# A Mamba-like block with mixture of experts: the token's row is made ready where x1 is made

## The chip, the cores and the metric

The kernel runs on one core of one Trainium2 chip, in float32. The metric is the device time of one execution in microseconds, as the median of the runs; smaller is better. The core has five instruction queues that run beside each other, each in its own fixed order: PE (matrix products), DVE and POOL (elementwise work; POOL also issues the indirect DMAs), ACT (functions, scale and bias) and SP (which only issues DMAs here).

## The reference, cut to what matters

Input are 8 sequences of 512 tokens with 256 features. For each sequence six modulation vectors of 256 numbers come from a small product. Two stages follow.

```python
sa, ca, ga, sb, cb, gb = mod vectors of the sequence      # ga, gb kept away from zero
h  = layernorm(x) * (1 + ca) + sa
x1 = x + ga * mixer(h)           # layernorm, W_in, causal conv + silu, linear state scan, gate, W_out, + h
h2 = layernorm(x1) * (1 + cb) + sb
logits = h2 @ wr + br            # 8 experts; top 1; gate = p1 / (p1 + p2)
y  = gelu(h2 @ w1[e] + b1[e]) @ w2[e] + b2[e]             # 256 -> 1024 -> 256, e the token's expert
out = x1 + gb * gate * y
```

The routing is dense in the reference (each expert over all tokens, masked); the kernel computes each token for its own expert alone.

## The kernel before, in words

**Order of the work.** All operations of a stage are first listed in a class `Plan` (lines 36 to 286). `Plan.order` then gives each engine one fixed order: always the operation that can start first by a table of estimated lengths (`length`), among equals the one with the earlier due time (`nc.due`); buffers are given in turn. `emit` issues them in that order. The recorded line of nearly every operation is therefore that of the plan's two helpers, L154 and L159, and operations are told apart by the names of their tiles.

**Stage 1** (lines 431 to 1138) goes over the 8 sequences b; a due time of 36 us per sequence (`PERIOD`) staggers them, so that several sequences overlap. A tile has 128 partitions; 512 tokens are 4 tiles.
- `stage_norm` (735): layer norm of x, modulation (h, on DVE), layer norm again, transposes to xnT (PE and ACT).
- `stage_base` (759): h times ga plus x, and W_out times ga (`wb_`): three 128x1024 operations on POOL.
- `stage_conv` (774): the scan's input pv and its three steps pd, each added to v by DVE; four products px, each copied to u and scaled to sv by ACT; three taps per product on DVE (`sv<-u,pt,sv`, twelve operations per sequence), then silu on ACT.
- `stage_out` (824): four products px for the gate (tz, tanh on ACT), the state's part pc (`v` times `cs`) added to sv by DVE, times the gate; then po (W_out and the router in one product, four tiles), x1 from po, statistics of x1 (`rs` by a power on POOL, `nm` on DVE), the logits, the choice of expert.
- `stage_place` (899): the gate's value, the token's row written to DRAM, and the token's number scattered into the list of its expert (`ids_d`, four indirect DMAs on POOL per sequence).

**The token's row.** `xp_d` in DRAM has one row per token, of `ROW` = 260 + 768 numbers (4112 bytes): x1 (256), rs, nm, gate, 0, and then copies of the sequence's three vectors for stage 2 (1 + cb, sb, gb), which SP copies in DRAM from `modb_d` for a whole sequence at a time (1.5 MB).

**Stage 2** (lines 1139 to 1332) works through slots of 256 tokens of one expert (12 pairs of tiles and 7 single tiles after 4 early slots; the rest behind a condition). Per slot: `name_tokens` (1023) loads the slot's token numbers, `expert_of` (1036) the expert's w1, b1, b2 and w2 (2.1 MB on SP), `rows_of` (1056) gathers the tokens' rows by an indirect DMA per tile on POOL, `features` (1066) computes h2 from the row (`hg`, three DVE operations per tile) and transposes it, `layer1` (1084) does ph and gelu, `layer2` (1260) does py and three DVE operations per tile, and an indirect DMA writes the output rows.

**The early slots.** When 6 sequences are routed, `early_table` (958) chooses 4 slots that are already full. Their token numbers are loaded in stage 1; the rows of slots 0 and 1 are gathered there, their transposed features made, and slot 0's weights loaded, so that `layer1` of slot 0 can follow the last po. The rows of slots 2 and 3 are gathered in stage 2. The table of the other slots is computed by some forty small DVE operations after the last sequence's routing; SP's next token list waits for it, and the weights of slots 2 and 3 stand behind that list in SP's queue.

Of the kernel before, what the change touches and what calls it, by code (L numbers as in the profile page):

```python
# [10 lines left out]
FP = mybir.dt.float32  # L11
# [10 lines left out]
OWN = 260  # L22
# [267 lines left out]
def adaln_mamba_moe_kernel(  # L290
# [89 lines left out]
    for e in range(E):  # L380
        nc.gpsimd.memset(seen[0:1, e : e + 1], float(e * TOK))
# [4 lines left out]
    for i in range(NSLOT):  # L386
        single = i >= NPAIR
        m = i - NPAIR if single else i
        for q, v in enumerate((
            m, NPAIR + m // 2 if single else m, (m % 2) * P if single else 0,  # L390
            0 if single else NSING,
        )):
            nc.gpsimd.memset(sl_at[:, q, i : i + 1], float(v))

    ex_at = cpool.tile([1, 2, 2 * E], FP, name="ex_at")
    for e in range(2 * E):
        nc.gpsimd.memset(ex_at[:, 0, e : e + 1], float(e % E))
        nc.gpsimd.memset(ex_at[:, 1, e : e + 1], float((e % E) * TOK))
# [5 lines left out]
    ROW = OWN + 3 * D  # L404
    ids_d = dpool.tile([NIDS, 1], I32, name="ids_d")
    id_views = dram_disjoint_views(ids_d, NB)
    xp_d = dpool.tile([TOK + BLK, ROW], FP, name="xp_d")
# [6 lines left out]
    xg0 = epool.tile([P, JB, ROW], FP, name="xg0", tag="xg0")  # L414
    zero = xg0[:, 0, :]
# [15 lines left out]
    with tc.tile_pool(name="wa", bufs=1) as wa, tc.tile_pool(  # L431
# [3 lines left out]
    ) as a2, tc.tile_pool(  # L435
        name="rowp", bufs=2
# [27 lines left out]
        cmt = wa.tile([DS, DI], FP, name="cmt")  # L464
# [5 lines left out]
        for j in range(JB):  # L470
            nc.sync.dma_start(out=xp_d[TOK + j * P : TOK + (j + 1) * P, :], in_=zero)
# [41 lines left out]
        def vectors():  # L513

            for half, to in ((0, mod_d), (1, modb_d)):
                mod = wa.tile([B, 3, D], FP, name=f"mod{half}", tag="mod")
                three(mod, sT, half, B)
                nc.sync.dma_start(out=to, in_=mod.rearrange("b i d -> b (i d)"))
# [71 lines left out]
        def states():  # L590
# [18 lines left out]
            lt = wa.tile([DS, CH, P], FP, name="lt")  # L609
# [70 lines left out]
        def stats(src, b, which, rs=None, nm=None):  # L680
# [8 lines left out]
            if rs is None:  # L689
                rs = sm.tile([P, NT], FP, name=f"rs{which}_{b}", tag=f"rs{which}", bufs=2)  # L690
                nm = sm.tile([P, NT], FP, name=f"nm{which}_{b}", tag=f"nm{which}", bufs=2)
# [82 lines left out]
        def stage_conv(t):  # L774
# [30 lines left out]
            sv = a2.tile([P, KI, L], FP, name="sv")  # L805
# [18 lines left out]
        def stage_out(t):  # L824
# [24 lines left out]

            xr = rowp.tile([P, NT, OWN], FP, name="xr")  # L850
            x1 = xr[:, :, 0:D]
            lg = sm.tile([P, NT, E], FP, name="lg")
            for n in range(NT):
                po = ps_o.tile([P, D + E], FP, name="po", tag="po")
                with nc.wanting([xr]):
# [13 lines left out]
            rs, nm = stats(x1, b, 2, xr[:, :, D], xr[:, :, D + 1])  # L869
# [27 lines left out]
            t.update(xr=xr, top=top, oh=oh)  # L897

        def stage_place(t):

            b, xr, top, oh = (t[k] for k in ("b", "xr", "top", "oh"))
# [3 lines left out]
            nc.vector.tensor_scalar(  # L905
                xr[:, :, D + 2], gt[:, :, 0], 0.5, 0.5, ALU.mult, ALU.add
            )
            nc.vector.memset(xr[:, :, D + 3 : OWN], 0.0)
            nc.sync.dma_start(
                out=xp_d[b * L : (b + 1) * L, 0:OWN].rearrange("(n p) c -> p n c", p=P), in_=xr  # L910
            )
            for n in range(b + 1 if b else 0, min(b + 2, B)):
                nc.sync.dma_start(
                    out=xp_d[n * L : (n + 1) * L, OWN:ROW], in_=modb_d[n].partition_broadcast(L)
                )

# [96 lines left out]
        def tiles(i):  # L1013
            return JB if i < NEARLY + NPAIR else 1
# [41 lines left out]
        def rows_of(i, xg, upto):  # L1056

            for j in range(tiles(i)):
                nc.gpsimd.indirect_dma_start(
                    out=xg[:, j, :], out_offset=None, in_=xp_d[0:upto, :],  # L1060
# [5 lines left out]
        def features(i, xg, hg, hT, tp):  # L1066

            mg = xg[:, :, OWN:ROW]
            for j in range(tiles(i)):
                nc.vector.tensor_scalar(  # L1070
                    hg[:, j, :], xg[:, j, 0:D], xg[:, j, D : D + 1], xg[:, j, D + 1 : D + 2],
                    ALU.mult, ALU.add,
                )
# [315 lines left out]
```

## Time and profile before

| | |
|---|---|
| runs | 588.8, 591.74, 591.7 us; median 591.7 |
| profiled execution | 587.33 us, its span 585.2 us |
| granted TensorE clock | 0.987 (mean over the span) |
| busy: PE, DVE, ACT, POOL | 562.3, 348.1, 211.0, 209.3 us |
| share of the chain that ended last | PE 73%, DMA 17%, DVE 3%, issue 3% |
| moved by DMA | 96.73 MB, 23.17 MB of it by POOL's queue (gathers, scatters) |
| po of the sequences begins at | 70.2, 105, 140, 173, 205, 238, 272, 305 us |

How to read it: the durations and the places come from the one profiled execution, whose time of 587.33 us is its span and what lies around it. An engine's row in a timeline gives the start, the duration, the engine, the line (a helper's), the operation with output and inputs, and in brackets how long the engine was idle before it and what released it. Operations of one engine overlap a little, so a row of a sequence is slightly longer than its share of the time. "sv" is also the buffer of y2; "h" that of the base; "xr" the row of x1 with rs, nm and gate.

### The profile page before, as it was taken

How to read it: one execution, taken by the hardware profiler on the slowest of the kernel's cores; microseconds unless marked ns; L12 is line 12 of the kernel's file. 1: busy time of each engine (PE TensorE's matmuls, PEld its weight loads, DVE VectorE, ACT ScalarE, POOL GpSimd, SP SyncE). 2: the span in 40 equal slices, each digit the busy share in tenths (PEclk: the TensorE clock that was granted, in tenths of full speed). 3: DMA queues.
4: the chain of work that ended last, by engine and by line, in shares of the span. 5: the costliest groups of instructions: out<-in, count | busy, mean ns of one | idle time of the engine just before them, and what ended most of it. 6: DMA issues, size and time to landing. Idle time of an engine off the chain costs nothing.

```text
span 585.2 us, 8673 instructions
## 1 busy us (share of the span) xinstructions
PE 562.3 (96%) x2882; PEld 428.0 (73%) x2882; DVE 348.1 (59%) x1087; ACT 211.0 (36%) x404; POOL 209.3 (36%) x330
## 2 busy tenths in 40 slices
PE   4999999999999999999999798999999999999996
PEld 2454766757576676757578687878988988988895
DVE  4879968798987968686595924163433433522312
ACT  2328454455363445252342021222422222332140
POOL 1423673635446372621333421342242222322112
PEclk9779999999999999999999999999999999999999
DMA  7348999420210101010553969997887787886000
GB/s 277 129 129 183 271 254 258 71 91 0 64 38 1 38 2 36 1 37 1 161 175 91 239 198 398 394 396 266 282 279 275 274 251 242 276 286 194 15 18 20
DMA packets 58703, 96.73 MB, mean 165 GB/s; under 512 B 9852, under 2 KB 41854, under 8 KB 58656
## 3 DMA queue, kind: packets, MB, share of 16 engines
q1 hardware_dynamic: 50720, 72.98, 41.4%
q0 software_dynamic: 7936, 23.17, 11.1%
q8 instruction: 24, 0.39, 0.3%
q14 instruction: 23, 0.19, 0.2%
HBM read 86.42 MB, written 22.81 MB: 187 GB/s over the span
## 4 chain that ended last, share of the span: by engine, by line
PE 73%; DMA 17%; DVE 3%; issue 3%; SPq 1%; POOL 1%; ACT 0%; POOLq 0%; ACTq 0%
PE py L154 10%; PE px L159 10%; PE po L154 9%; PE px L154 9%; DMA out<-ot,ids 8%; PE ph L159 6%; PE ph L154 6%; PE pc L154 3%; PE po L159 3%; PE pd L154 3%; DMA ids<-ids_d 3%; DMA ids_d<-tok,row 2%; DMA w1t<-in_w 2%; PE py L159 2%; DMA xg<-xp_d,ids 1%
## 5 line engine op out<-in xcount | busy, mean ns | idle before, releaser
L159 ACT ACTIVATE gl<-ph,b1t 128x256 f32<-128x256 f32 (+1 forms) x152 | 68.3, 452 | 179.5 <-PE ph L154 159.9
L154 PE MATMUL py<-w2t,gl 128*128 128x256 f32 x476 | 108.3, 379 | 0.0
L154 PEld LDWEIGHTS py<-w2t,gl 128*128 128x128 f32 x476 | 90.4, 190 | 12.3
L159 PE MATMUL ph<-hT,w1t 128*128 128x256 f32 (+1 forms) x304 | 84.1, 358 | 5.4 <-DMA w1t<-in_w 3.0
L154 PE MATMUL ph<-hT,w1t 128*128 128x256 f32 (+1 forms) x304 | 83.8, 357 | 0.0
L159 POOL DMA_INDIRECT out<-ot,ids x36 | 36.4, 1012 | 130.7 <-DVE ot L159 121.0
L159 DVE TENSOR_TENSOR ot<-py,b2t 128x256 f32<-128x256 f32 x34 | 14.4, 424 | 113.0 <-PE py L154 113.0
L159 DVE SCALAR_TENSOR_TENSOR sv<-u,pt,sv 128x512 f32<-128x512 f32 x96 | 71.9, 759 | 4.3 <-ACT sv L159 4.3
L159 POOL DMA_INDIRECT xg<-xp_d,ids x36 | 38.9, 1080 | 87.3 <-DMA ids<-ids_d 48.3
L159 PE MATMUL px<-xnT,wi 128*128 128x512 f32 x128 | 69.6, 625 | 0.0
L154 PE MATMUL px<-xnT,wi 128*128 128x512 f32 x128 | 66.2, 599 | 0.0
L159 PEld LDWEIGHTS ph<-hT,w1t 128*128 128x128 f32 x304 | 54.4, 190 | 12.2 <-issue 3.6
L154 PEld LDWEIGHTS ph<-hT,w1t 128*128 128x128 f32 x304 | 55.3, 190 | 6.2
L154 PEld LDWEIGHTS px<-xnT,wi 128*128 128x128 f32 x128 | 24.6, 192 | 31.2 <-issue 31.2
L159 POOL DMA_INDIRECT ids_d<-tok,row x32 | 34.5, 1077 | 24.2 <-DVE row L159 13.2
L159 ACT COPY u<-px 128x512 f32<-128x512 f32 x32 | 18.7, 585 | 67.0 <-PE px L154 66.4
L159 ACT ACTIVATE tz<-px 128x512 f32<-128x512 f32 x32 | 19.0, 595 | 51.1 <-PE px L154 50.3
L159 POOL TENSOR_TENSOR rs<-ve,nhalf 128x4 f32<-128x4 f32 x16 | 18.8, 1174 | 44.9 <-DVE ve L159 32.2
L159 PEld LDWEIGHTS px<-xnT,wi 128*128 128x128 f32 x128 | 21.3, 192 | 17.4 <-issue 16.5
L159 DVE COPY hT<-tp 128x512 f32<-128x512 f32 (+1 forms) x20 | 12.7, 634 | 35.4 <-PE tp L154 27.4
L159 DVE TENSOR_TENSOR xr<-po,h 128x256 f32<-128x256 f32 x32 | 13.5, 423 | 30.6 <-PE po L154 30.4
L159 DVE TENSOR_TENSOR hg<-hg,xg 128x256 f32<-128x256 f32 x72 | 29.3, 421 | 1.1
(347 smaller groups left out, 949.8 us busy)
## 6 DMA issues: line engine op xcount, KB each, us to landing
w1t<-in_w SPq DMA_DIRECT2D x19, 1024.0 KB
w2t<-in_w SPq DMA_DIRECT2D x19, 1024.0 KB
xp_d<-modb_d SPq DMA_DIRECT2D x8, 1536.0 KB
xp_d<-xr SPq DMA_DIRECT2D x8, 520.0 KB
xt<-in_x SPq DMA_DIRECT2D x8, 512.0 KB
bc<-mod_d SPq DMA_DIRECT2D x7, 384.0 KB
b2t<-in_b SPq DMA_DIRECT2D x19, 128.0 KB
w<-in_w SPq DMA_DIRECT2D x2, 1024.0 KB
```

The costliest lines, as they stand in the source:

```text
L154: me["calls"].append(lambda: getattr(getattr(self.nc, name), op)(*args, **kw))
L159: calls=[lambda: getattr(getattr(self.nc, name), op)(*args, **kw)],
```

## The change

The row becomes three times 256 numbers (3072 bytes): x1, h2, and gate times gb. It is made in stage 1:

- `stage_place` writes x1 by itself, loads the sequence's three vectors into all partitions (`bb`, 384 KB), and makes h2 (four ACT operations `normed` of 128x256, then two POOL operations of 128x1024: times 1 + cb, plus sb) and gate times gb (`gg`, four ACT operations). Both lie in the buffer of `sv`, which has a pool of its own now and is held until the two rows are written. Their due time is a period later.
- The last sequence's two writes are issued in stage 2, behind the weights of slot 1.
- The copies of vectors in DRAM are gone.
- `features` transposes from the gathered row; `hg` is gone. `layer2` does two DVE operations of 128x512 per slot ahead of py (gate gb b2, added to x1), and two per tile after it.
- The rows of all four early slots are gathered in stage 1, one after the other on POOL.
- Constant tables come from counters and copies in place of single memsets; some small tiles change their pools; `layer1` of slot 0 is due a period earlier.

```diff
-    ROW = OWN + 3 * D
-    xp_d = dpool.tile([TOK + BLK, ROW], FP, name="xp_d")
+    xp_d = dpool.tile([TOK + BLK, 3 * D], FP, name="xp_d")
...
+        name="yp", bufs=2
+    ) as yp, tc.tile_pool(
...
-            sv = a2.tile([P, KI, L], FP, name="sv")
+            sv = yp.tile([P, KI, L], FP, name="sv")
...
-            b, xr, top, oh = (t[k] for k in ("b", "xr", "top", "oh"))
+            b, sv, x1, rs, nm, top, oh = (
+                t[k] for k in ("b", "sv", "x1", "rs", "nm", "top", "oh")
+            )
+            own = xp_d[b * L : (b + 1) * L].rearrange("(n p) (i d) -> i p n d", p=P, i=3)
+            nc.sync.dma_start(out=own[0], in_=x1)
             gt = sm.tile([P, NT, 1], FP, name="gt")
             nc.vector.tensor_tensor(gt, top[:, :, 0:1], top[:, :, 1:2], ALU.subtract)
             nc.scalar.activation(gt, gt, AF.Tanh, scale=0.5)
-            nc.vector.tensor_scalar(
-                xr[:, :, D + 2], gt[:, :, 0], 0.5, 0.5, ALU.mult, ALU.add
-            )
-            nc.vector.memset(xr[:, :, D + 3 : OWN], 0.0)
+            nc.vector.tensor_scalar(gt, gt, 0.5, 0.5, ALU.mult, ALU.add)
...
+            h2, gg = (
+                sv[:, k * KD : (k + 1) * KD, :].rearrange("p k l -> p (k l)").rearrange(
+                    "p (n d) -> p n d", n=NT
+                ) for k in range(2)
+            )
+            bb = rowp.tile([P, 3, D], FP, name="bb", bufs=1)
             nc.sync.dma_start(
-                out=xp_d[b * L : (b + 1) * L, 0:OWN].rearrange("(n p) c -> p n c", p=P), in_=xr
-            )
-            for n in range(b + 1 if b else 0, min(b + 2, B)):
-                nc.sync.dma_start(
-                    out=xp_d[n * L : (n + 1) * L, OWN:ROW], in_=modb_d[n].partition_broadcast(L)
-                )
+                out=bb, in_=modb_d[b].rearrange("(i d) -> i d", d=D).partition_broadcast(P)
+            )
+
+            nc.due += PERIOD
+            normed(h2, x1, rs, nm)
+            nc.gpsimd.tensor_tensor(h2, h2, rows(bb[:, 0, :]), ALU.mult)
+            nc.gpsimd.tensor_tensor(h2, h2, rows(bb[:, 1, :]), ALU.add)
+            if b < B - 1:
+                nc.sync.dma_start(out=own[1], in_=h2)
+            for n in range(NT):
+                nc.scalar.activation(
+                    gg[:, n, :], bb[:, 2, :], AF.Identity, scale=gt[:, n, :]
+                )
+            if b < B - 1:
+                nc.sync.dma_start(out=own[2], in_=gg)
+            else:
+                late.extend(((own[1], h2), (own[2], gg)))
+            nc.due -= PERIOD
...
-        def features(i, xg, hg, hT, tp):
-            mg = xg[:, :, OWN:ROW]
+        def features(i, xg, hT, tp):
             for j in range(tiles(i)):
-                nc.vector.tensor_scalar(
-                    hg[:, j, :], xg[:, j, 0:D], xg[:, j, D : D + 1], xg[:, j, D + 1 : D + 2],
-                    ALU.mult, ALU.add,
-                )
-                nc.vector.tensor_tensor(hg[:, j, :], hg[:, j, :], mg[:, j, 0:D], ALU.mult)
-                nc.vector.tensor_tensor(hg[:, j, :], hg[:, j, :], mg[:, j, D : 2 * D], ALU.add)
                 for k in range(KD):
                     nc.tensor.transpose(
-                        tp[:, k, j * P : (j + 1) * P], hg[:, j, k * P : (k + 1) * P], ident
+                        tp[:, k, j * P : (j + 1) * P], xg[:, j, 1, k * P : (k + 1) * P], ident
                     )
...
+                for i in range(NEARLY):
+                    pre.append(rows_of(
+                        i, epool.tile([P, JB, 3, D], FP, name=f"xg_{i}", tag=f"xg{i}"), (b + 1) * L
+                    ))
                 for i in range(2):
...
-                    pre.append(rows_of(
-                        i, epool.tile([P, JB, ROW], FP, name=f"xg_{i}", tag=f"xg{i}"), (b + 1) * L
-                    ))
...
-        nc.due = (B + 4) * PERIOD
+        nc.due = (B + 3) * PERIOD
...
         got = [slot0, fetched(1, pre[1])]
+        for to, v in late:
+            with nc.wanting(done=[got[1][4]]):
+                nc.sync.dma_start(out=to, in_=v)
...
+            nc.vector.tensor_tensor(
+                ot[:, 0:jb], gg, b2t.unsqueeze(1).to_broadcast([P, jb, D]), ALU.mult
+            )
+            nc.vector.tensor_tensor(x1, x1, ot[:, 0:jb], ALU.add)
             for j in range(tiles(i)):
...
-                nc.vector.tensor_tensor(ot[:, j, :], py, b2t, ALU.add)
-                nc.vector.tensor_tensor(ot[:, j, :], ot[:, j, :], mg[:, j, 2 * D : 3 * D], ALU.mult)
-                nc.vector.scalar_tensor_tensor(
-                    ot[:, j, :], ot[:, j, :], xg[:, j, D + 2 : D + 3], xg[:, j, 0:D],
-                    ALU.mult, ALU.add,
-                )
+                nc.vector.tensor_tensor(ot[:, j, :], py, gg[:, j, :], ALU.mult)
+                nc.vector.tensor_tensor(ot[:, j, :], ot[:, j, :], x1[:, j, :], ALU.add)
...
-        got += [fetched(i, None, [ids[:, NEARLY, :]]) for i in range(2, NEARLY)]
+        got += [fetched(i, pre[i], [ids[:, NEARLY, :]]) for i in range(2, NEARLY)]
```

## The prediction

> **What bounds the kernel now.** I read the page first (busy shares, slices, chain), then a table of stretches, then the engines' timelines. PE is busy 562.3 of 585.2 us, and the table shows where it is not:
>
> ```profile
> core 0: us, PE busy (x) PEld busy (x) DVE busy (x) ACT busy (x) POOL busy (x), PEclk, DMA share, GB/s
> ...
> 140.00:173.00 33.00, 33.00 (x179) 22.53 (x178) 29.92 (x93) 15.77 (x29) 16.30 (x26) 1.00 0.15 45
> ...
> 206.00:239.00 33.00, 32.99 (x177) 22.45 (x176) 24.99 (x77) 15.72 (x29) 15.59 (x27) 1.00 0.06 17
> ...
> 315.00:330.00 15.00, 14.01 (x69) 12.04 (x67) 11.92 (x74) 3.89 (x9) 8.90 (x9) 1.00 0.87 263
> 330.00:345.00 15.00, 12.79 (x61) 10.83 (x62) 8.28 (x26) 3.47 (x8) 3.86 (x4) 1.00 0.71 126
> ```
>
> Two things are to be seen. From 105 us to the end of stage 1 PE has no hole to speak of, so nothing taken off another engine there can shorten the run; but DVE is at 25 to 30 of 33 us, so something put on DVE can lengthen it. The only holes of some size that the change can reach lie at the passage to stage 2, where PE waited three times:
>
> ```profile
> 329.94 0.67 PE L159 MATMUL ph<-hT,w1t 128*128 128x256 f32 x2 [0.99 <-DMA w1t<-in_w]
> 335.84 0.70 PE L159 MATMUL ph<-hT,w1t 128*128 128x256 f32 x2 [2.21 <-ACT gl L159]
> 356.88 0.67 PE L159 MATMUL ph<-hT,w1t 128*128 128x256 f32 x2 [2.04 <-DMA w1t<-in_w]
> ```
>
> The second is a DMA too: ACT's gelu had waited for the bias b1t. From 390 to 570 us PE is full (180.00 of 180.00).
>
> **The change, gains first.** PE's instructions stay. *Passage.* The gathers of slots 2 and 3 (before issued at 314.75 to 320.7, 2.1 MB) move into stage 1, behind those of slots 0 and 1; the weights of slot 1, issued at 319.06, then have the DMA to themselves: the 0.99 and 2.21 us go. Transposes no longer wait for DVE's hg and what followed it at 383 to 388 (0.3 + 0.8 us). The wait of 2.04 us for slot 3's weights I keep: they follow the late table, its token list and slot 2's weights on SP, and the table's last operations now also follow slot 0's output operations on DVE; it may go, or double. A routing matmul (pk) stands earlier in PE's queue, some 0.3 us to pay. *Tail.* After the last py (579.45) DVE does two operations instead of three: 0.48 us (row: the scaled add, 482 ns). Sum: 0.99 + 2.21 + 1.1 + 0.48 - 0.3 = 4.5 us gained, bounds 0.5 and 6.5.
>
> *What is worth nothing.* Stage 2's DVE work per slot falls from 5.8 to 3.7 us: PE covers it. Gathers of 3072 instead of 4112 bytes and no copies of modulation rows (8 x 1.5 MB, which fill the DMA at 0.94 to 0.98 in 45 to 105 us): PE's losses there, 1.7 us, are mostly startup waits for small tables, not these; 0 to 0.5 us, taken as 0. Some 100 memsets of 89 ns leave POOL's idle time. Per sequence SP now issues x1, the load bb, h2 and gg (1.9 MB) for 2.0 MB before: DMA share there is 0.05 to 0.26, hidden.
>
> *ACT.* Eight 128x256 operations per sequence: the row xn<-h,nm,rs x4 is 2.08 us, so 4.2 us on top of about 16 of 33. They stand between the copies of px, where ACT idled 0.45 us between pairs and 2.4 us before the first tz; what PE needs next (u, tz) is late by at most one of them. Nothing, or 0.5 us a sequence if that cover is gone.
>
> *POOL.* Two 128x1024 operations of 2.36 us per sequence (h2 times, plus), 4.7 us, on 16 of 33. By itself this fits. Behind them stand the four scatters of token numbers, 1 to 3 us later, which nobody needs but the early table of sequence 5 (ids issued at 279.22, some 2 us late, slot 0 not before 314) and of sequence 7. All eight early gathers (1.3 us apart) stand before h2 of sequence 6, which so comes at 295 to 300; SP, in order, holds slot 0's weights behind that write, to 300 instead of 292.21. They took about 12 us and are wanted at 314: 2 us of cover.
>
> **What decides: where POOL's new operations fall.** Before, POOL's 128x1024 operations lie beside po, when DVE mostly reads PSUM. Where one does meet a DVE operation with two operands in SBUF, the timelines of POOL and DVE show this:
>
> ```profile
> 64.20 2.36 POOL L159 TENSOR_TENSOR h<-h,bc 128x1024 f32<-128x1024 f32 x1 [0.56 <-ACT xn L159]
> 117.56 2.64 POOL L159 TENSOR_TENSOR wb__431<-wo,bc 128x1024 f32<-128x1024 f32 x1
> 149.97 2.36 POOL L159 TENSOR_TENSOR wb__507<-wo,bc 128x1024 f32<-128x1024 f32 x1
> ```
>
> ```profile
> 64.77 0.69 DVE L159 TENSOR_TENSOR sv<-sv,pc 128x512 f32<-128x512 f32 x1 [0.21 <-PE pc L154]
> 65.38 1.72 DVE L159 SCALAR_TENSOR_TENSOR sv<-tz,sv 128x512 f32<-128x512 f32 x1
> 117.89 2.34 DVE L159 SCALAR_TENSOR_TENSOR xr<-mv,xr 128x4 f32<-128x4 f32 x1
> 150.73 2.67 DVE L159 TENSOR_TENSOR h<-xn,bc 128x1024 f32<-128x1024 f32 x1
> ```
>
> An operation on four elements, otherwise 0.15 us, took 2.34 us and ended just when POOL's did (120.2); the one at 65.38, otherwise 0.68, lasted until 66.56 + 0.6; the one at 150.73, otherwise 1.21, until 152.33 + 1.1. The one at 64.77 with pc from PSUM was not held up. The Trainium skill has this as a rule (SBUF — State Buffer, "Who interferes with whom"): a VectorE instruction with two SBUF inputs and a GpSimd instruction that reads SBUF share a port, and whichever comes second is blocked for the whole of the first. It speaks against this change, and the group's row would hide it:
>
> ```profile
> L159 DVE SCALAR_TENSOR_TENSOR sv<-u,pt,sv 128x512 f32<-128x512 f32 x96 | 71.9, 759 | 4.3 <-ACT sv L159 4.3
> ```
>
> By this mean of 759 ns the convolution's twelve operations cost after what they cost before, and the sum is -4.5 us, 587. By the rule each of POOL's two h2 operations takes up to 2.36 us out of DVE if it starts among them. In the changed kernel's instruction order it does: ACT makes h2's norm behind nm and the gate's tanh, some 10 us after po, and POOL's pair follows at once; DVE is then at the seventh or eighth of the twelve. I take the rule's value, as the near rows show it whole.
>
> Followed through once, for the sequence whose po ended at 213.3 (times of before):
>
> ```profile
> 226.28 0.27 DVE L159 TENSOR_TENSOR v<-v,pd 32x120 f32<-32x120 f32 x1
> ...
> 230.15 0.23 DVE L159 TENSOR_TENSOR v<-v,pd 32x96 f32<-32x96 f32 x1
> ```
>
> ```profile
> 228.45 0.35 PE L159 MATMUL pd<-v,lm 32*32 32x96 f32 x2
> ...
> 231.59 0.39 PE L159 MATMUL pc<-v,cs 128*128 128x128 f32 x2
> ```
>
> ACT ends px's last pair at 223.0, tanh and three norms by 224.9; POOL multiplies from about 225.4 (a running DVE operation ends first) to 227.8, adds to 230.2. Between, DVE gets one operation in at most. So v<-v,pd moves from 226.5 to 231.2, and PE, which wants it for pd at 228.45, stands 2.75 us. Three statistics operations of h now stand ahead of the convolution instead of behind it (two more, 0.7 us): 3.4 us. The next sum of v (234.7) then just meets pc, but y2's last operations end some 0.6 us after PE's last cover before po: 4.0. So 2.75 to 4.0 us in which PE is idle; I take the middle, 3.4. In the fuller stretch from 140 the slack was less (v's last sum ended at 164.0, pc began at 164.43), in the one from 281 some DVE work on hg is gone but the pair falls on the last four of the twelve. So 3.4 us for each of six sequences, 20.4. The first has its routing ahead of its convolution and scatters between the two POOL operations: 0.5. The last collides with the tables of stage 2, whose end waits for py anyway: 0.
>
> **Sum.** 20.4 + 0.5 - 4.5 = +16.4 us. Its base is the profiled execution (587.33 us, of which the span is 585.2); the median of the runs shown is 591.7, 4.4 above, and the difference is carried over: 608.1, 2.8% slower.
>
> **Rivals.**
> *A, the likeliest (0.73):* the block stands, 608. With 2 us per sequence (the pair starts later and meets PSUM operations) 599.5; with all 4.7 us lost and little gained at the passage, 617. Its own range is 599 to 617.
> *B, no block that PE feels (0.13):* POOL's operations wait in DVE's gaps, or DVE catches up. For it: the DVE gap of 1.10 us before pc at 232.75, and that at 117.56 POOL itself waited 0.29 us. Against: in three rows above POOL was never put off longer. It decides if DVE is held under about 2 us before v's second sum (226.5 against 228.45); then the passage's gain stays: 591.7 - 4.5 = 587.
> *C, half of it (0.09):* one of the two operations is caught by slack, 1 us per sequence: 6 + 0.5 - 4.5 = +2, 594, and 591 to 599 with its bounds.
> *D, another slower cause (0.05):* h2 of sequence 6 is so late that slot 0's weights come after 314; the cover of 2 us gone, PE waits some 5 us at the first ph, on top of B or C: 592 to 599. For it: SP's fixed order. Against: the 14 us between issue and need.
> That the change misses its aim at the passage (weights again behind a token list) costs A 2 to 4 us, inside its range.
>
> **Numbers.** Less than 0.5% (3 us) can't be told from no change here. Faster: B, 0.13. The same: a third of C and of D, 0.05. Slower: 0.82. The range leaves out B and the top of A: 592 to 617.
>
> **What would show it.** Right: several sv<-u,pt,sv of 2.4 to 3 us beside POOL's sv<-sv,bb, the group's mean above 0.9 us; PE idle some 3 us before pd or pc in each stage-1 sequence, put down to DVE v; po every 36 to 37 us instead of 33.4; POOL's rows of 128x1024 at about 2.36; no waits at the first ph of slot 1. Wrong: a po period near 33.4, with sv<-u at 759 ns, or PE's idle time put down to ACT or to weights.

## The result, and the profile after

The changed kernel takes 622.4 us (median of four runs, 619.7 to 630.7) beside 590.3 us for the kernel before (585.7 to 591.7): a ratio of 1.054, 95% interval 1.045 to 1.064. The forecast was 608, with a range of 592 to 617. One of the four runs (630.7) fell in a slower state of the chip; such runs are left out of the ratios here and below, though not out of the medians. The direction was right; the loss is twice the one forecast. The profiled execution took 620.29 us, its span is 618.6 us, 33.4 us longer than before's 585.2.

First the page's busy times and slices, of before and then of after (each digit is a fortieth of the span; PEclk is the granted TensorE clock in tenths):

```profile
PE 562.3 (96%) x2882; PEld 428.0 (73%) x2882; DVE 348.1 (59%) x1087; ACT 211.0 (36%) x404; POOL 209.3 (36%) x330
...
PE   4999999999999999999999798999999999999996
...
PEclk9779999999999999999999999999999999999999
```

```profile
PE 578.4 (93%) x2882; PEld 437.4 (71%) x2882; DVE 362.6 (59%) x979; ACT 239.1 (39%) x468; POOL 253.3 (41%) x246
...
PE   5999988968989999899996989999999999999996
...
PEclk9669989989989989899997989999999999999999
```

The same 2882 matmuls keep PE busy for 578.4 us instead of 562.3. So the 33.4 us are two things: 17.3 us more in which PE has nothing to do, and 16.1 us by which the same instructions take longer. The PEclk row says when: behind startup the clock is below 9 in seven slices, and in six of these the PE row is below 9 too (in the seventh lies the wait of 1.49 us at 217.66).

Cut at the first and the last start of po (startup, stage 1, the rest), the table of stretches reads, before and after:

```profile
core 0: us, PE busy (x) PEld busy (x) DVE busy (x) ACT busy (x) POOL busy (x), PEclk, DMA share, GB/s
0.00:70.19 70.19, 60.87 (x314) 34.34 (x315) 54.71 (x174) 30.40 (x53) 24.99 (x59) 0.90 0.66 197
70.19:304.83 234.64, 233.05 (x1231) 157.99 (x1231) 183.35 (x596) 106.84 (x190) 108.04 (x198) 1.00 0.30 79
304.83:585.20 280.37, 268.35 (x1338) 235.71 (x1338) 110.04 (x318) 73.73 (x163) 76.24 (x73) 1.00 0.69 229
```

```profile
0.00:69.22 69.22, 61.44 (x307) 34.43 (x307) 55.34 (x175) 28.48 (x50) 20.21 (x50) 0.85 0.32 109
69.22:341.85 272.63, 248.78 (x1244) 165.97 (x1243) 223.92 (x587) 133.03 (x248) 155.78 (x125) 0.95 0.36 77
341.85:618.60 276.75, 268.15 (x1335) 237.05 (x1334) 83.35 (x218) 77.62 (x171) 77.34 (x71) 0.99 0.70 224
```

Stage 1 is 38.0 us longer, the rest 3.6 us shorter, startup 1.0 shorter. In stage 1 PE's idle time goes from 1.6 us (234.64 less 233.05) to 23.9, and its busy time from 233.1 to 248.8. Two of the stretches that the prediction showed, answered by the table of after:

```profile
140.00:173.00 33.00, 30.72 (x169) 21.58 (x169) 27.06 (x82) 18.03 (x35) 18.84 (x16) 1.00 0.33 88
206.00:239.00 33.00, 31.26 (x168) 22.16 (x168) 26.63 (x72) 16.65 (x32) 20.20 (x16) 0.95 0.34 54
```

The longest of PE's waits in stage 1 and behind it, from PE's timeline of after:

```profile
88.30 0.38 PE L157 MATMUL pk<-oh,lower 128*128 128x32 f32 x2 [1.52 <-DVE oh L157]
...
135.73 0.60 PE L157 MATMUL pd<-v,lm 32*32 32x120 f32 x2 [4.78 <-DVE v L157]
...
179.11 0.41 PE L152 MATMUL pk<-sx,ones 128*128 128x32 f32 x2 [2.08 <-DVE sx L157]
...
254.18 0.41 PE L152 MATMUL pk<-sx,ones 128*128 128x32 f32 x2 [2.50 <-DVE sx L157]
...
333.70 0.77 PE L157 MATMUL pc<-v,cs 128*128 128x128 f32 x2 [4.75 <-DVE v L157]
...
358.72 0.20 PE L157 MATMUL prun_l<-seen,ones 128*1 128x8 f32 x2 [1.94 <-DVE seen L157]
```

All are put down to DVE. What held DVE at 254 us is in the timelines of POOL and DVE:

```profile
248.77 5.35 POOL L157 TENSOR_TENSOR sv<-sv,bb 128x1024 f32<-128x1024 f32 x2 [6.34 <-ACT sv L157]
```

```profile
248.26 0.73 DVE L157 SCALAR_TENSOR_TENSOR sv<-u,pt,sv 128x512 f32<-128x512 f32 x1
248.93 2.32 DVE L157 TENSOR_TENSOR sx<-sx,oh 128x8 f32<-128x8 f32 x1
251.18 0.73 DVE L157 SCALAR_TENSOR_TENSOR sv<-u,pt,sv 128x512 f32<-128x512 f32 x1
251.84 2.29 DVE L157 TENSOR_TENSOR sx<-sx,oh 128x8 f32<-128x8 f32 x1
```

Two sums of 128x8, otherwise 0.15 us, last 2.3 us each, one inside each of POOL's two operations: 4.3 us taken out of DVE, and PE, which wants that sx for pk, stands 2.50 us, and 0.52 more at the next pd. That is the mechanism of the forecast, in the sequence it was followed through for and nearly at the size given there (2.75 to 4.0 us). The victim is another one: PE stands at pk for sx, not at pd for v. Over the run 15 of POOL's 16 new operations hold one DVE operation each for 2.0 to 2.8 us longer than it usually takes, 32.6 us in all. Only three of the 15 belong to the convolution; eleven are small ones of 128x4 or 128x8, so the convolution's group hides most of it:

```profile
L157 DVE SCALAR_TENSOR_TENSOR sv<-u,pt,sv 128x512 f32<-128x512 f32 x96 | 81.9, 862 | 3.4 <-ACT sv L157 3.3
...
L157 POOL TENSOR_TENSOR sv<-sv,bb 128x1024 f32<-128x1024 f32 x16 | 42.6, 2662 | 32.2 <-ACT sv L157 31.7
```

The group's mean is 862 ns, 10 us in all above before's 759. I had asked for above 900.

How the clock falls, from the table of stretches around the wait of 4.78 us that ends at 135.73:

```profile
125.00:130.00 5.00, 5.00 (x24) 2.85 (x24) 4.97 (x6) 2.51 (x5) 4.90 (x3) 1.00 0.22 84
130.00:135.00 5.00, 0.95 (x3) 0.12 (x1) 5.00 (x15) 2.73 (x5) 1.49 (x2) 0.85 0.35 105
135.00:140.00 5.00, 4.27 (x10) 2.33 (x11) 5.00 (x12) 2.37 (x6) 3.77 (x2) 0.50 0.01 3
140.00:145.00 5.00, 3.92 (x19) 2.12 (x18) 5.00 (x9) 2.19 (x5) 1.95 (x3) 0.97 0.30 105
```

In 135 to 140 PE is busy again, at half the clock: a px group of x2 that takes 1.0 to 1.1 us takes 2.08:

```profile
136.98 2.08 PE L157 MATMUL px<-xnT,wi 128*128 128x512 f32 x2
```

The clock record of the trace has seven such stretches between startup and tail, of 3.4 us (at 89.1, 181.3, 218.8, 256.4, 358.8) or 6.8 us (133.5, 331.5); before has none there. What lies of the six in stage 1 on work is 4 x 3.4 and 2 x 4.6 us, 22.8 us at half speed, so some 11 us of the 15.7. Another 1.2 us, estimated from their mean lengths before, are twelve transposes more that fall between the first and the last po; the remaining 3 to 4 us I can't place.

### The profile page after: what moved, and what is told of

The parts are those of the page before. It is cut to its first block, busy times and chain, and to the rows that moved or that the text cites. A ratio compares the mean times of both kernels' runs of the same rounds, so it can differ in the third digit from the quotient of the medians.

```text
span 618.6 us, 8620 instructions
## 1 busy us (share of the span) xinstructions
PE 578.4 (93%) x2882; PEld 437.4 (71%) x2882; DVE 362.6 (59%) x979; ACT 239.1 (39%) x468; POOL 253.3 (41%) x246
## 4 chain that ended last, share of the span: by engine, by line
PE 53%; DVE 20%; DMA 17%; issue 4%; POOL 3%; ACT 1%; SPq 1%; POOLq 0%; DVEq 0%; ACTq 0%
PE py L152 11%; DVE sv L157 9%; DMA out<-ot,ids 8%; PE ph L157 7%; PE ph L152 7%; PE po L152 6%; PE px L157 4%; PE px L152 4%; DMA xp_d<-sv 3%; DVE sx L157 3%; PE pc L152 2%; DMA w1t<-in_w 2%; DMA ids_d<-tok,row 2%; PE po L157 2%; PE py L157 2%
## 5 line engine op out<-in xcount | busy, mean ns | idle before, releaser
L157 POOL DMA_INDIRECT out<-ot,ids x36 | 37.7, 1046 | 127.2 <-DVE ot L157 116.7
L157 DVE TENSOR_TENSOR ot<-py,xg 128x256 f32<-128x256 f32 x36 | 15.3, 424 | 126.4 <-PE py L152 120.0
L157 DVE SCALAR_TENSOR_TENSOR sv<-u,pt,sv 128x512 f32<-128x512 f32 x96 | 81.9, 862 | 3.4 <-ACT sv L157 3.3
L157 PE MATMUL px<-xnT,wi 128*128 128x512 f32 x128 | 72.5, 649 | 1.3 <-DVE sv L157 1.2
L152 PE MATMUL px<-xnT,wi 128*128 128x512 f32 x128 | 70.5, 634 | 0.0
L157 POOL TENSOR_TENSOR rs<-ve,nhalf 128x4 f32<-128x4 f32 x24 | 31.1, 1295 | 60.8 <-DVE ve L157 55.0
L157 POOL TENSOR_TENSOR sv<-sv,bb 128x1024 f32<-128x1024 f32 x16 | 42.6, 2662 | 32.2 <-ACT sv L157 31.7
L157 POOL DMA_INDIRECT ids_d<-tok,row x32 | 36.8, 1149 | 18.5 <-issue 6.4
L157 PEld LDWEIGHTS px<-xnT,wi 128*128 128x128 f32 x128 | 21.5, 196 | 19.4 <-issue 14.9
L157 DVE TENSOR_TENSOR x<-po,h 128x256 f32<-128x256 f32 x32 | 13.4, 420 | 29.5 <-PE po L152 26.0
L157 ACT ACTIVATE tz<-px 128x512 f32<-128x512 f32 x32 | 18.8, 590 | 30.5 <-PE px L152 21.5
```

The source lines that it names most:

```text
L152: me["calls"].append(lambda: getattr(getattr(self.nc, name), op)(*args, **kw))
L157: calls=[lambda: getattr(getattr(self.nc, name), op)(*args, **kw)],
```

## The experiments

All on the kernel after unless said otherwise. Theory P is the forecast's: POOL's two h2 operations hold DVE. The rivals are ACT's eight new operations (A), the new order of DVE's and PE's work (O), and SP's and the DMA's new transfers, with the buffers that wait for them (T). Ratios are to the kernel before, run beside it on the same chip.

**POOL's pair left out.**

```diff
             normed(h2, x1, rs, nm)
-            nc.gpsimd.tensor_tensor(h2, h2, rows(bb[:, 0, :]), ALU.mult)
-            nc.gpsimd.tensor_tensor(h2, h2, rows(bb[:, 1, :]), ALU.add)
```

> The changed kernel without the two POOL operations that multiply and add the modulation (h2 is written as the bare norm); everything else stays, the eight ACT operations, the row's writes, the early gathers. Theory P (POOL's reads block DVE, PE waits for DVE's v, and the granted clock falls after each such wait): po to po back to about 33.5 us, no half-clock stretch in stage 1, span 581 to 585 us (585.2 of before, less what the passage gains), some 5.5% under the changed kernel. Theory A (the eight ACT operations stand in the way): hardly faster than the changed kernel, 610 us or more. Theory D (the different order of DVE's own operations): between, 600 to 612 us.

599.6 us, ratio 1.019 (1.014 to 1.024). Of the 5.4% the pair is worth 3.5 points, about 21 us. The rest, 1.9%, is something else, against the theory that the pair is all of it. Its trace shows three things that are left. POOL's older 128x1024 operations now make ten DVE operations between 60 and 365 us longer by more than 0.7 us, 16.3 us in all, where before's did it to five, 7.9 us. The buffer of sv is held until the row's writes have landed, and ACT waits for that:

```profile
122.46 0.78 ACT L157 ACTIVATE sv<-px,pt 128x512 f32<-128x512 f32 x1 [5.70 <-DMA xp_d<-sv]
```

And at the passage PE waits for weights that SP issues right behind the late token list (354.67 and 355.82 us):

```profile
361.19 1.19 PE L157 MATMUL ph<-hT,w1t 128*128 128x256 f32 x2 [5.04 <-DMA w1t<-in_w]
```

**ACT's eight operations left out.**

```diff
-            normed(h2, x1, rs, nm)
-            nc.gpsimd.tensor_tensor(h2, h2, rows(bb[:, 0, :]), ALU.mult)
+            with nc.wanting(done=[nm]):
+                nc.gpsimd.tensor_tensor(h2, x1, rows(bb[:, 0, :]), ALU.mult)
...
-            for n in range(NT):
-                nc.scalar.activation(
-                    gg[:, n, :], bb[:, 2, :], AF.Identity, scale=gt[:, n, :]
-                )
```

> The changed kernel without the eight ACT operations per sequence: POOL multiplies x1 itself by the vector and adds the other, and gate times gb is not computed (the third part of the row gets what lies in the buffer). Both POOL operations stay. Theory P: still slow, 605 to 625 us. Theory A: 585 to 592 us.

628.0 us, ratio 1.068 (1.061 to 1.075): not faster. The pair starts earlier in it, right behind nm, and meets other DVE operations. ACT is not what holds the kernel back while the pair is there.

**Does POOL hold DVE because it is busy, or because it reads?** The pair replaced by fills of the same tile, which read nothing; four of 0.96 us a sequence:

```diff
-            nc.gpsimd.tensor_tensor(h2, h2, rows(bb[:, 0, :]), ALU.mult)
-            nc.gpsimd.tensor_tensor(h2, h2, rows(bb[:, 1, :]), ALU.add)
+            def filled(h2=h2):
+                for v in (0.5, 0.25):
+                    chip.gpsimd.memset(h2, v)
+            for _ in range(2):
+                plan.call("gpsimd", filled, [h2], [h2], 2.45)
```

> The changed kernel with each of the two POOL operations replaced by two fills of the same 128x1024 tile: POOL is busy about as long at the same places, but reads nothing from SBUF (h2 is a constant). Theory P in the form of a shared read path: as without POOL's operations, 581 to 588 us, and DVE's sv<-u,pt,sv near 0.75 us beside the fills. Theory O (POOL being busy is what costs: scatters and buffer preparations late): as the changed kernel, 610 to 622 us. If fills block DVE too, also 610 to 622, and the long DVE rows stay.

604.8 us, ratio 1.029 (1.022 to 1.035): above the expected 581 to 588, because the kernel without the pair is already at 599.6 (which I had not yet separated), and some 5 us above that. The lines that bear on the question, from the groups:

```profile
L157 DVE SCALAR_TENSOR_TENSOR sv<-u,pt,sv 128x512 f32<-128x512 f32 x96 | 71.3, 760 | 2.9 <-ACT sv L157 2.8
...
L935 POOL MEMSET sv<- 128x1024 f32 x32 | 30.7, 960 | 40.2 <-ACT sv L157 39.3
```

With 30.7 us of POOL's writes the convolution is at 760 ns, before's 759. That mean alone would be a weak witness (without the pair and without fills it is 789). Operation by operation it is clear: 81 DVE operations overlap a fill, and one of them is longer than usual by more than 0.7 us (a CAST of 128x4 at 343.78, 1.00 us), against 15 of 44 beside the pair. It is POOL's reading that holds DVE. (The rule of the Trainium skill that the forecast weighed, SBUF — State Buffer, "Who interferes with whom", says this too: it names a GpSimd instruction that reads SBUF.)

**The pair on DVE itself.**

```diff
-            nc.gpsimd.tensor_tensor(h2, h2, rows(bb[:, 0, :]), ALU.mult)
-            nc.gpsimd.tensor_tensor(h2, h2, rows(bb[:, 1, :]), ALU.add)
+            nc.vector.tensor_tensor(h2, h2, rows(bb[:, 0, :]), ALU.mult)
+            nc.vector.tensor_tensor(h2, h2, rows(bb[:, 1, :]), ALU.add)
```

> The changed kernel with the two 128x1024 operations on DVE in place of POOL (1.22 us each by the rows of h<-xn,bc), where the plan puts them behind the convolution and the last sum of v, ahead of the sums with pc. Theory P: DVE loses 2.4 us per sequence in place of 4.7, at a place with 1 to 2.5 us of slack: 0 to 1.5 us of PE wait per sequence, too short for the clock to fall, so 582 to 594 us. Theory A: still 610 us or more. Theory D: 600 us or more.

609.1 us, ratio 1.037 (1.032 to 1.042): better than on POOL (16 operations of 1.21 us, 2.4 us a sequence, instead of up to 4.7 of DVE's time), but DVE has no room for those either. The 582 to 594 expected took the rest of the change as free.

**The pair alone, put into the kernel before.** It reads and writes spare tiles; nothing else is changed:

```diff
+            nc.due += PERIOD
+            with nc.wanting(done=[gt]):
+                nc.gpsimd.tensor_tensor(spare, xr[:, :, 0 : D - 2], wo[:, :, 0 : D - 2], ALU.mult)
+            nc.gpsimd.tensor_tensor(spare, spare, wo[:, :, 0 : D - 2], ALU.add)
+            nc.due -= PERIOD
```

> The kernel before with two POOL operations of 128x1016 added per sequence (x1 times and plus a constant, into a tile that nobody reads), listed where the changed kernel lists h2; nothing else is changed. Theory P (POOL's reads block DVE): each pair takes 4.7 us out of DVE among the convolution's operations, PE waits 2 to 4 us per sequence for v and the clock falls after most of these waits: 600 to 615 us against some 588. Theory D (the changed kernel is slow by the new order of its own instructions, POOL's pair only finds it full): 588 to 594 us.

640.5 us, ratio 1.096 (1.089 to 1.104), more than expected. In stage 1 the forecast's mechanism is complete (POOL, DVE, PE):

```profile
243.66 2.32 POOL L159 TENSOR_TENSOR spare<-xr,wo 128x1016 f32<-128x1016 f32 x1
246.06 2.65 POOL L159 TENSOR_TENSOR spare<-spare,wo 128x1016 f32<-128x1016 f32 x1
```

```profile
243.62 2.41 DVE L159 TENSOR_TENSOR add<-add,rsum 128x32 f32<-128x32 f32 x1
...
246.62 2.14 DVE L159 TENSOR_TENSOR lg<-lg,add 128x32 f32<-128x32 f32 x1
```

```profile
252.25 0.63 PE L159 MATMUL pk<-oh,lower 128*128 128x32 f32 x2 [3.88 <-DVE oh L159]
```

Stage 1 goes from 234.6 to 267.1 us: idle 21.5, busy 245.6. So the pair alone does nearly all that the whole change does there. The excess is at the passage, where PE waits 12.08 us for slot 1's bias b1t and 4.5 us more for hg and hT: perhaps because POOL's gathers, still at the passage here, come late; that isn't shown.

**The row without h2 and gate product: x1 is written three times.** ACT's and POOL's new operations are gone, the transfers' sizes stay:

```diff
+            for k in range(1, 3):
+                if b < B - 1:
+                    nc.sync.dma_start(out=own[k], in_=x1)
+                else:
+                    late.append((own[k], x1))
```

> The changed kernel without any computing of h2 and gate times gb: the three parts of the row are three writes of x1. No new ACT and no new POOL operation is left; early gathers, the loads, the writes, the tables and the order the plan makes of the rest stay. Without POOL's pair alone the time was 599.6 us. If ACT's eight operations are the rest of the loss: 583 to 587 us. If the rest is the new order (routing's pk earlier in PE's queue, the old POOL operations beside other DVE work, startup): 594 to 600 us.

594.7 us, ratio 1.012 (1.002 to 1.021). Against the run without the pair (1.019) that is some 0.7 points, 4 to 5 us; the intervals (1.014 to 1.024 there) overlap over most of their length. Nor would it be ACT's operations alone: the rows are written from x1 here, so sv's buffer is not held, and the wait of 5.70 us above is gone. About 7 us are left in which neither ACT nor POOL has anything new. The trace shows PE standing at 117.59, at po, while 3072-byte packets of bb's loads (one row of modulation vectors copied to 128 partitions) occupied the DMA from about 102 to 120 us, many of them 1 to 3 us long instead of the 0.12 to 0.2 usual. But nothing reads bb in this kernel, so nothing holds its loads back: all eight are issued between 70.9 and 102.0 us, where the changed kernel issues one per sequence (71.7, 106.4, 148.0 us and so on).

**The same without the load of bb.**

```diff
-            bb = rowp.tile([P, 3, D], FP, name="bb", bufs=1)
-            nc.sync.dma_start(
-                out=bb, in_=modb_d[b].rearrange("(i d) -> i d", d=D).partition_broadcast(P)
-            )
```

> The run with three writes of x1 (594.7 us), and beside its other omissions (no h2, no gate product) the load of bb, the sequence's three modulation rows copied to 128 partitions, is left out too; nothing else differs. Theory T (this load, whose packets took up to 1 to 3 us each around 105 to 131 us, holds up the other transfers, and through DVE's wait at 117 us PE) expects 587 to 590 and no PE wait beside a late transfer in 70 to 130 us. The rival (the rest is the changed order of DVE's work in a sequence, norm operations and sums of oh ahead of the convolution) expects 593 to 597.

587.6 us, ratio 1.0044 (1.0014 to 1.0074), as expected of the load. The table of stretches over the place, first with the load and then without:

```profile
115.00:120.00 5.00, 2.66 (x10) 2.11 (x10) 1.47 (x6) 0.00 (x0) 0.93 (x1) 0.82 0.75 50
120.00:125.00 5.00, 5.00 (x15) 2.87 (x15) 3.43 (x9) 1.25 (x2) 3.93 (x3) 0.84 0.77 217
```

```profile
115.00:120.00 5.00, 5.00 (x13) 2.25 (x12) 3.02 (x13) 2.42 (x4) 2.89 (x2) 1.00 0.88 69
120.00:125.00 5.00, 5.00 (x25) 2.71 (x23) 5.00 (x13) 2.53 (x4) 2.15 (x2) 1.00 0.97 275
```

With the loads PE stood for 2.3 us and then ran below full clock; without, neither. So eight loads in one bunch delay PE there. What one load per sequence costs in the changed kernel this pair of runs does not say, and the ratios (1.002 to 1.021 and 1.001 to 1.007) overlap; stage 1 is 7.4 us shorter without the loads, by one execution of each. Slow packets are also not the load's alone: the stretch from 115 to 120 without it has the DMA busy at 0.88 with 69 GB/s. The new order (rival O) with the early gathers, as the planner makes it of what is left here, comes to 0.4%, at most 0.7%.

In this run, in the one before and in the one without the pair the passage gains nothing: PE waits 4.74, 4.83 and 5.04 us for the weights behind the token list, with half clock for 6.8 us, and the time behind the last po is 280.1 to 280.2 us beside before's 280.4.

**The gathers of slots 2 and 3 put back at the passage.**

```diff
-                for i in range(NEARLY):
+                for i in range(2):
                     pre.append(rows_of(
...
-        got += [fetched(i, pre[i], [ids[:, NEARLY, :]]) for i in range(2, NEARLY)]
+        got += [fetched(i, None, [ids[:, NEARLY, :]]) for i in range(2, NEARLY)]
```

> The changed kernel with the gathers of early slots 2 and 3 back at the passage to stage 2, where the kernel before has them. If moving them gained what I reckoned (the waits for slot 1's weights and bias, 3.2 us): 3 us slower than the changed kernel, 623 to 628 us, with a wait for w1t of slot 1 in the trace. If nothing: 618 to 623 us.

625.4 us, ratio 1.068 (1.060 to 1.076). From the last po to the end it takes 283.1 us instead of after's 276.8, with three new waits, of 1.37, 1.58 and 1.58 us, of tp for the gathered rows, and 6.8 us at half clock from 384.8. The whole runs alone could not tell this (the intervals, 1.045 to 1.064 and 1.060 to 1.076, overlap); the stretch and its waits do. Moving the gathers pays in this kernel, 6.3 us by one execution of each where I gave the weights 3.2. But the wait expected, for slot 1's weights, isn't there: PE waits for the late rows themselves. So the price that I gave the gathers' share of the DMA isn't shown.

**One gather moved in the kernel before, nothing else of the change.**

```diff
+                for i in range(3):
+                    pre.append(rows_of(
+                        i, epool.tile([P, JB, ROW], FP, name=f"xg_{i}", tag=f"xg{i}"), (b + 1) * L
+                    ))
...
-        cmt = wa.tile([DS, DI], FP, name="cmt")
+        cmt = a3.tile([DS, DI], FP, name="cmt", tag="tz")
```

> The kernel before with one part of the change alone: the gather of slot 2's rows moved into stage 1 behind those of slots 0 and 1 (slot 3's stays, there is no room for its rows; the tables cmt, lt and mod take their place in other buffers, as in the changed kernel, to make room). The whole row and POOL's pair are not in it. My step on the passage (the 2.1 MB gathered ahead of slot 1's weights cost 4.5 us, both slots together) expects half of that, 1.5 to 3 us below before, with PE's waits at 329.9 and 335.8 us (0.99 and 2.21) gone or halved: 583 to 586 beside a before of 586. The rival (the weights are late for another reason, their own 2 MB a slot) expects 586 to 588.

614.6 us, ratio 1.048 (1.042 to 1.053), and it says nothing on the question. The shared buffers made the planner order the startup anew. DVE now stood 24.80 us for a sequence's x, whose load stands behind 10.5 MB of modulation copies on SP's queue, with the operation that PE wanted in DVE's queue behind it. From the timelines of DVE and PE:

```profile
127.52 0.43 DVE L159 BATCH_NORM_STATS2 st<-xt 128x6 f32<-128x256 f32 x1 [24.80 <-DMA xt<-in_x]
```

```profile
128.99 1.25 PE L154 MATMUL po<-wb__279,sv 128*128 128x264 f32 x2 [21.97 <-DVE sv L159]
```

The waits for slot 1's weights at the passage are gone in it, as expected; one of 5.10 us for the next slot's hg has come in their place.

**Does a wait by itself slow PE down?** The kernel before, with 22 to 42 multiplications by one put on DVE between a slot's transposed rows and its first layer, for seven slots of stage 2, far from POOL's and ACT's work of stage 1:

```diff
+        LATE = {6: 22, 7: 25, 8: 28, 9: 31, 10: 34, 11: 38, 12: 42}
...
+                    for _ in range(LATE[i]):
+                        chip.vector.tensor_scalar(
+                            hT[:, :, 0:n], hT[:, :, 0:n], 1.0, None, ALU.mult
+                        )
```

> The kernel before, with PE held up in stage 2, seven times, by DVE multiplying a slot's transposed features by one 22, 25, 28, 31, 34, 38 and 42 times over, unknown to the plan; at about 0.35 us each and with some 7 us of slack this should make PE wait from under 1 us to about 8 us. Theory C (a PE wait of about 2 us or more brings the granted clock to half for about 3.4 or 6.8 us after it): half-clock stretches in stage 2 behind the longer waits, none behind those under 1 us, and PE's busy time up by half of their length. Rival (the clock fell for something in stage 1): no half-clock stretch in stage 2, PE busy as before, 562 us.

633.4 us in one run. From the table of stretches around the first of the waits, 5.33 us:

```profile
417.00:422.00 5.00, 5.00 (x25) 4.36 (x24) 4.62 (x12) 2.84 (x6) 0.82 (x1) 1.00 0.92 280
422.00:427.00 5.00, 0.62 (x5) 0.36 (x3) 4.62 (x12) 0.47 (x1) 0.00 (x0) 0.95 0.89 296
427.00:432.00 5.00, 4.05 (x10) 3.27 (x11) 4.79 (x11) 0.47 (x1) 0.98 (x1) 0.50 0.08 31
```

Five waits (5.33, 6.34, 7.30, 4.94 and 11.19 us) and five stretches at half clock (6.8, 6.8, 6.8, 3.4 and 10.2 us), one with each, which begins during the wait or just behind it; PE's busy time is 573.9 us, 11.6 more than before, 2.3 us a wait. This is the second half of the loss, without any of the change. (Of the seven hold-ups two gave no wait of this size.)

**POOL's pair held back to the next sequence's po**, where DVE mostly reads PSUM (on the variant with late gathers; a third buffer for sv; two of the eight sequences left as they were):

```diff
-            nc.gpsimd.tensor_tensor(h2, h2, rows(bb[:, 0, :]), ALU.mult)
-            nc.gpsimd.tensor_tensor(h2, h2, rows(bb[:, 1, :]), ALU.add)
...
+            def rest(done=()):
+                with nc.wanting(done=done):
+                    nc.gpsimd.tensor_tensor(h2, h2, rows(bb[:, 0, :]), ALU.mult)
+                nc.gpsimd.tensor_tensor(h2, h2, rows(bb[:, 1, :]), ALU.add)
...
+                if n == 0 and held:
+                    held.pop()([x1[:, 0, :]])
```

> The run with the gathers of slots 2 and 3 late (625.4 us), with POOL's two h2 operations of a sequence, and the writes of h2 and of the gate product, held back until the next sequence's first sum of po and base (not for sequences 5 and 7), so that they should fall where DVE reads PSUM. A third buffer for sv keeps h2 until then. All the work is still done. Theory P (it is the meeting with DVE's two-operand operations that costs) expects the twelve sv<-u operations back at 760 to 790 ns in the mean and 603 to 612 us. The rival (POOL's volume of work, or the writes, cost the time wherever they fall) expects 620 to 628.

623.3 us, ratio 1.061 (1.053 to 1.068), against 1.068 with the pair in its old place: no gain that can be told, and theory P's 603 to 612 missed, as its 760 to 790 ns for the convolution (844). DVE's timeline shows one reason:

```profile
123.74 2.31 DVE L157 SCALAR_TENSOR_TENSOR nm<-mv,rs 128x4 f32<-128x4 f32 x1
126.08 2.33 DVE L157 TENSOR_TENSOR add<-nm,rsum 128x32 f32<-128x32 f32 x1
128.34 2.89 DVE L157 SCALAR_TENSOR_TENSOR sv<-u,pt,sv 128x512 f32<-128x512 f32 x1
```

POOL's second operation (123.41, 2.62 us) and its old work behind it now meet the routing's first steps, and PE stands 4.10 us for v at 134.27. The window beside po is narrower than what POOL has to put there; twelve DVE operations are held beside the pair. Stage 1 is 3.5 us shorter than with the pair in its old place (267.2 against 270.7), and the time behind the last po 5.2 us longer (288.3 against 283.1). So the run refutes my estimate of the room, not that reading holds DVE.

**Stage 1 over the runs**, PE's busy and idle time between the first and the last po, from the tables of stretches (us):

| kernel | busy | idle |
|---|---|---|
| before | 233.1 | 1.6 |
| x1 three times, no bb | 233.6 | 2.5 |
| x1 three times | 238.9 | 4.6 |
| after without the pair | 239.3 | 9.0 |
| fills in its place | 241.6 | 15.2 |
| the pair on DVE | 243.7 | 16.6 |
| late gathers, the pair beside po | 246.2 | 21.0 |
| before with the pair | 245.6 | 21.5 |
| late gathers | 248.0 | 22.7 |
| after | 248.8 | 23.9 |
| after without ACT's operations | 248.1 | 24.0 |
| before with one gather moved | 237.9 | 27.0 |

The matmuls are nearly the same in all (1231 before, 1244 in after). The busy time rises with the idle time; in the rows of 9 us and more by 0.6 to 0.8 us for each us of idle time that came on top of before's. The last row is the exception, 0.2: nearly all of its idle time is the one wait of 21.97 us, and most of its stretch at half clock lies in that wait. For each us of idle time, many short waits cost more than one long one.

## Why the prediction was wrong in size

*"PE's instructions stay"* is the step that failed. They do, but the sum took from it that their time stays too. In stage 1 they take 15.7 us more, some 11 us of it because around waits the clock falls to half for 3.4 or 6.8 us. The forecast gave this term nothing and no reason. With it the sum is 608.1 + 15.7 = 623.8; measured 622.4, which is this close by luck, since other terms were wrong and cancel. The hold-ups in stage 2 show it without the change. The Trainium skill names the effect (TensorE: Matmul & The Clock Gate, "HAM oscillation — how this bites in real kernels"): no PE-idle gaps above about 3.4 us. The forecast's waits (2.75 to 4.0, in the middle 3.4) lie on both sides of that figure, so the page leaves open whether they bring it. The runs are stricter: every wait of 2.28 us or more behind startup, in all runs, came with such a stretch, and so did many of 1.3 to 2.2 us. The measurement decides, and it should have sent me to the row of PEclk with a question.

*The pair's block, 20.4 us in six sequences.* The mechanism is shown from both sides (taken away, and put alone into the kernel before). The total of idle time fits by luck. Waits that follow directly on a meeting of pair and DVE are, in the sequences 2 to 7 of the eight, 1.57, 2.60, 1.49, 3.02, 0 and 4.75 us: 13.4 us, 2.2 us each where I took 3.4. In size the sequence followed through was right (3.02 against 2.75 to 4.0), by way of the routing's sums where the forecast had the convolution and v.

*The first sequence, 0.5, and pk's earlier place, 0.3:* 1.52 us at pk and 1.16 at px. The one at pk is in the run without the pair too (88.20), so it belongs to the new order. *The last, 0:* at 356.35 the sum seen<-sx,oh was held for 2.31 us, and PE waited 1.94 at 358.72; py did not cover it. *The transfers, hidden:* not all of them. In after ACT's first copy into sv waited twice until the row's write had left that buffer:

```profile
124.42 0.78 ACT L157 ACTIVATE sv<-px,pt 128x512 f32<-128x512 f32 x1 [1.84 <-DMA xp_d<-sv]
242.40 0.78 ACT L157 ACTIVATE sv<-px,pt 128x512 f32<-128x512 f32 x1 [2.14 <-DMA xp_d<-sv]
```

Bytes and DMA share (0.05 to 0.26) were the wrong measure: at 108 to 117 us single packets of the write and of bb's load took up to 6.8 us. The price of these waits was not isolated. *ACT, 0 or 0.5 a sequence:* open; the medians (594.7 against 599.6) would allow the alternate, 4 us, but the intervals overlap and sv's buffer is free in the faster run. The wait of 4.78 us at 135.73, where no operation of the pair ran, is not explained in full: its sequence's convolution began behind the ACT wait at 124.42, and POOL's old h operations (128.53, 2.34 us) met DVE's work anew.

*The passage, -4.5:* 276.75 against 280.37, so -3.6, with the last sequence's 1.94 in it. The size is right, and so is the place: no wait at the first ph of slot 1; one of 1.37 us is left for weights at 392.79. But it holds for this slow stage 1: in the three runs without the pair weights were late again, as the forecast had allowed for at the end of its rivals, and nothing was gained.

*Po every 36 to 37 us:* every 34.1 to 43.7, 38.9 in the mean. *Rival B* (no block that PE feels) is refuted by the kernel before with the pair alone. *Rival C* took 1 us per sequence; the 2.2 measured lie between it and A. *Rival D* (slot 0's weights late) did not come: ph of slot 0 waits for nothing.

What stays open: 3 to 4 us of stage 1's slower PE that the clock's stretches and the added transposes don't cover; how the 1.9% without the pair divide between POOL's older operations, sv's buffer, ACT and the loads; and why the pair in the kernel before costs 12 us at b1t. No version tried is faster than the kernel before.

## What to carry to other kernels

Where one engine sets the end, price a new wait on it twice: its length, and what the engine loses afterwards at a lower clock; compare busy time at an equal number of instructions to see the second. Before work goes onto GpSimd, ask what two-input or copying work VectorE has in SBUF in the same microseconds, the smallest operations included, since each can be held for a whole GpSimd operation. And a buffer that is newly held until a write to DRAM has landed is to be judged by the slowest packets of that write, not by its bytes.

## What was not expected of the hardware

The half-clock stretches behind startup come in multiples of 3.4 us (3.4, 6.8, 10.2, once 23.9, cut off only by the end of the run). All waits of PE of 2.28 us and more behind startup had one, over all runs; the shortest wait that stood alone and had one was 1.33 us (at 92.76 in the run with x1 written three times), and three waits of 0.33, 0.50 and 0.99 us within 4 us had one as well (before 210.0, the pair on DVE). Between 1.3 and 2.2 us some waits had one and some, such as before's 2.21 and 2.04 at the passage, had none: the length of a wait alone doesn't decide.

VectorE operations with a single tensor input are held by GpSimd too. In after, beside POOL's pair (136.15 to 141.74 and 327.53 to 332.65):

```profile
136.46 2.31 DVE L157 TENSOR_SCALAR gt<-gt 128x4 f32<-128x4 f32 x1
...
330.37 2.30 DVE L157 CAST row<-rowf 128x4 int32<-128x4 f32 x1
```

Both are otherwise 0.15 us. And packets of the load of one 3072-byte row to 128 partitions were slow in two of after's eight loads (0.79 us in the mean at 112 to 122 us, 0.75 at 223 to 230) where the other six have 0.17 to 0.21. The 1024-byte packets of the row's write beside the first of these were slow too, up to 6.7 us, so it is not this kind of load alone. What makes them slow stays open.
